# Small work of a graph kernel's last attention batch placed in pieces, its closing stage scaled two batches ahead, and the last batch normalised by halves

## The chip, the cores and the metric

The kernel runs on one core of a Trainium2 chip. The core has five engines that run side by side, each with its own instruction stream: TensorE (PE, matrix products; its weight loads are listed as PEld), VectorE (DVE), ScalarE (ACT), GpSimd (POOL) and SyncE (SP), which here only issues transfers. Sixteen DMA engines move data between HBM and the on-chip memory (SBUF); products of PE land in PSUM, a small second memory whose banks have to be freed before PE can write them again. Engines wait for one another through semaphores.

The metric is the device time of one execution in microseconds (us). Where several runs are given, it is their median.

## The reference

There are B = 16 batches of N = 1024 nodes with C = 256 features, all in fp32, and one dense adjacency matrix of 1024 x 1024. The computation has two layers, each with a residual and a layer normalisation over the features. Cut to what matters:

```python
# layer 0: graph-weighted queries, four heads of attention
g    = relu(einsum('bcn,bnm->bcm', fea, adj * A_s) * para)   # queries
k, v = split(x @ kv_w)
attn = softmax(q @ k.T * scale)                              # per head, 1024 x 1024
x    = layernorm(x + attn @ v)

# layer 1: graph convolution, two linear maps with batch norm
A_hat = normalise(adj + I)                                   # by degrees
agg   = einsum('nm,bmd->bnd', A_hat, x)
h     = relu(batchnorm(agg @ W1.T + b1))                     # statistics over all batches
out   = batchnorm(h @ W2.T + b2)                             # statistics over all batches
x     = layernorm(x + out)
```

The second batch norm needs its statistics over all sixteen batches before any batch can be finished. So the closing stage, which scales, adds the residual, normalises and stores, begins only when the last batch's second linear map is done.

## The kernel before

**How it is tiled.** A batch's features are a tile of 128 partitions x 8 node blocks x 256 features. Attention scores are made transposed, for two heads at a time, as tiles `ps` of 128 keys x 1024 (two heads x 512 queries). ACT makes `p` of them with an exponential, DVE adds up `acc` (the softmax's denominator), and PE multiplies `p` with `v` into `po`.

**What sets the order.** On PE, ACT and DVE the order of instructions is that of the program text (`manual_schedule`). On POOL and SP a scheduler orders what the text issues. In the attention, work is cut into *bursts* of two score tiles: in burst u of batch b (16 bursts in a batch) PE makes the scores of burst u, then `back(j - 1)` makes the products `po` of the burst before, with the DVE sums of `acc`. What follows in the burst is other work, in three kinds of lists:

- `sums`, the denominators of two heads (`normalise`): PE product `den`, ACT copy, two small transfers out to HBM and back as columns `dcol`.
- `full`, the residual of half the queries of two heads (`residual`): DVE reciprocal, PE transposes `poT`, DVE product `o`, POOL addition into `x`.
- `late`, the layer norm of a finished batch: `statistics_x1` (8 pairs of `bn_stats` and `bn_aggr` on DVE, then four POOL steps that give `rs_l` and `nm_l`) and `finish_x1` (8 ACT operations, line 622, then POOL issues the store to `x1_d`).

In the last batch, b = 15, there is no following batch whose queries could be prepared. Its bursts hold what the next layer needs (table `last`): transposes of the adjacency (`pah`, copied by ACT to `ahT`), loads and transposes of the weights (`pw1`, `pw2`, copied by DVE to `w12T`), node degrees (`dg`), whose inverse root makes a round trip through HBM to become `dinv_row`, and DVE's scaling of the adjacency rows with it (line 1107). The text also loads there the first batches of layer 0's result, `x1l_0` and `x1l_1`. Those take slots of the three-slot pool `xp`, and `x1l_1` gets the slot of batch 14's `x`. After the last burst PE goes over to the first aggregation, `pagg` (line 1134).

The transposes `pw`, `pah`, `poT` and `den` take turns in two PSUM banks (`tile_t`); `po` takes turns in two others, which are free when ACT's copy and DVE's addition into `oT` (lines 962, 963) are done.

**The closing stage.** `o2T[b]` holds batch b's output of the second linear map, with channels on partitions, in two blocks c. `batchnorm` gives the closure `coefficients` that makes scale `sg` and shift `sh` of one block: one DVE step and five POOL steps. Then, for each batch:

- `scale_shift(b)`: ACT scales and shifts `o2T[b]`, in place (line 1594).
- `residual2(b)`: PE transposes it back. Node blocks 0 to 3 go to PSUM tiles `pf` and DVE adds the residual; for blocks 4 to 7, PE itself adds the residual, in PSUM tiles `held`, of which there are three. DVE takes statistics of all eight blocks, and ten small operations on POOL (on DVE for the last batch) make `rstd` and `nmr` in a tile `w_l`.
- `finish(b)`: DVE normalises blocks 0 and 1, ACT blocks 4 to 7, 2 and 3; SP issues the store, and then loads the residual of a later batch into the freed place.

The loop runs `residual2(b)`, `scale_shift(b + 1)`, `finish(b - 1)`.

Of the kernel before, what the change touches and what calls it, by code (L numbers as in the profile page):

```python
# [18 lines left out]
P = 128  # L19
# [496 lines left out]
def fast_path(  # L516
# [87 lines left out]
    def layernorm_steps(t, name):  # L604


        st = small.tile([P, NCH, 6], F32, tag="ln_st", name=f"st_{name}")
        mv = small.tile([P, NCH, 2], F32, tag="ln_mv", name=f"mv_{name}")
        rstd = small.tile([P, NCH], F32, tag="ln_rs", name=f"rs_{name}")
        nmr = small.tile([P, NCH], F32, tag="ccol", name=f"nm_{name}")  # L610

        def statistics():
            for n in range(NCH):
                nc.vector.bn_stats(st[:, n, :], t[:, n, :])
                nc.vector.bn_aggr(mv[:, n, :], st[:, n, :])
            rsqrt(rstd, mv[:, :, 1], EPS)
            nc.gpsimd.tensor_tensor(nmr, mv[:, :, 0], rstd, ALU.mult)
            nc.gpsimd.tensor_scalar(nmr, nmr, -1.0, None, ALU.mult)  # L618

        def apply():  # L620
            for n in range(NCH):
                nc.scalar.activation(  # L622
                    t[:, n, :], t[:, n, :], AF.Identity,
                    bias=nmr[:, n : n + 1], scale=rstd[:, n : n + 1],
                )

        return statistics, apply
# [97 lines left out]
    with (  # L725
# [286 lines left out]

        def statistics_x1(b):
            statistics, st[b]["ln"] = layernorm_steps(st[b]["x"], f"l0_{b}")
            statistics()

        def finish_x1(b):
            s = st.pop(b)
            s["ln"]()
            nc.gpsimd.dma_start(x1_d[b], s["x"])  # L1020

# [20 lines left out]

        def transpose_weights():
            t = pap.tile([P, CC, N], F32, tag="pa", name="w12T")
            wl["w1T"] = t[:, 0, :].rearrange("p (c f) -> p c f", f=FH)
            wl["w2T"] = t[:, 1, :].rearrange("p (k c) -> p k c", c=C)
            for c in range(CC):
                pt = tile_t(f"pw1_{c}")
                for r in range(HC):
                    nc.tensor.transpose(  # L1050
                        pt[:, r * P : (r + 1) * P], wl["w1"][:, r, c * P : (c + 1) * P], ident
                    )
                nc.vector.tensor_copy(wl["w1T"][:, c, :], pt)
            for pair in range(HC // 2):
# [98 lines left out]
        with tc.manual_schedule(engines={mybir.EngineType.PE, mybir.EngineType.Activation, mybir.EngineType.DVE}):  # L1153
# [35 lines left out]
            for u, todo in (  # L1189
                (1, (load_weights,)), (6, (load_x1l, 0)), (9, (degrees,)), (10, (transpose_weights,)),  # L1190
                (12, (add_identity,)), (13, (load_x1l, 1)), (14, (scale_adjacency, 0)),
                (14, (scale_adjacency, 1)),
            ):
                last.setdefault(u, []).append((todo[0], todo[1:]))
            before_last = {
                8: [(adjacency_rows, (n,)) for n in (0, 1, 2, 3)],
# [6 lines left out]
            for j in range(len(bursts)):  # L1203
# [11 lines left out]
                if b == B - 1:  # L1215
                    if u == 0:
                        run(sums, 1)
                    elif u in (2, 9, 13):
                        run(full, 2)
                    elif u == 8:  # L1220
                        run(sums, 1)
                    elif u == 11:
                        run(late, 1)
                    elif u == 12:
                        run(late, 1)
                elif u == 0:
# [58 lines left out]

    def batchnorm(stats, gamma, beta, k, name):

# [5 lines left out]
        def coefficients(j):  # L1293
            g, s = sg[:, j : j + 1], sh[:, j : j + 1]
            nc.vector.bn_aggr(mv[:, j, :], stats[:, j].rearrange("p a s -> p (a s)"))
            rsqrt(g, mv[:, j, 1:2], EPS)
            nc.gpsimd.tensor_tensor(g, g, gamma[:, j : j + 1], ALU.mult)
            nc.gpsimd.tensor_tensor(s, mv[:, j, 0:1], g, ALU.mult)
            nc.gpsimd.tensor_tensor(s, beta[:, j : j + 1], s, ALU.subtract)

# [199 lines left out]
    with tc.tile_pool(name="hl", bufs=2) as hl, tc.tile_pool(name="o2p", bufs=1) as o2p:  # L1500
# [9 lines left out]

        coefficients2, sg2, sh2 = batchnorm(bn2_st, cols["g2"], cols["be2"], CC, "bn2")
        hs_of = {0: h0}
# [61 lines left out]
        with (  # L1574
# [14 lines left out]

            def scale_shift(b):  # L1590
                for hs in (H0, H1) if b == 0 else (slice(0, N),):
                    for c in range(CC):
                        o = o2T[b][:, c, hs]
# [14 lines left out]

            def residual2(b, between):
                xt = xf[b]  # L1610
                st = small.tile([P, NCH, 6], F32, tag="ln_st", name=f"st_l1_{b}")
                for pair in range(2):
# [10 lines left out]
                    for n in (2 * pair, 2 * pair + 1):  # L1623
                        nc.vector.bn_stats(st[:, n, :], xt[:, n, :])
                for pair in range(2, 4):
                    if b:
# [10 lines left out]
                for n in range(4, NCH):  # L1637
                    nc.vector.bn_stats(st[:, n, :], held[b][:, (n - 4) * C : (n - 3) * C])
                if b == B - 1:
                    between()  # L1640

                me, qe, mo, qo = (st[:, :, k] for k in (1, 2, 4, 5))
                w = small.tile([P, 4, NCH], F32, tag="ln_w", name=f"w_l1_{b}")
                rstd, nmr, dif, var = (w[:, k, :] for k in range(4))
                pool = nc.vector if b == B - 1 else nc.gpsimd
                pool.tensor_tensor(nmr, me, mo, ALU.add)
# [5 lines left out]
                pool.tensor_tensor(var, var, dif, ALU.add)  # L1652
                nc.gpsimd.tensor_tensor(rstd, var, mhalf, ALU.pow)
                pool.tensor_tensor(nmr, nmr, rstd, ALU.mult)
                pool.tensor_scalar(nmr, nmr, -0.5, None, ALU.mult)
                return rstd, nmr

            def finish(b, rstd, nmr):
                xt, hx = xf.pop(b), held.pop(b)
                y = o2T[b].rearrange("p c n -> p (c n)").rearrange("p (n c) -> p n c", c=C)  # L1660
                last = b == B - 1
                for n in (0, 1, 2, 3) if last else (0, 1):
                    nc.vector.tensor_scalar(
                        y[:, n, :], xt[:, n, :], rstd[:, n : n + 1], nmr[:, n : n + 1],
                        ALU.mult, ALU.add,
                    )
                for n in (4, 5, 6, 7) if last else (4, 5, 6, 7, 2, 3):
                    nc.scalar.activation(  # L1668
# [15 lines left out]
            add_x1(0, 3)  # L1684
            scale_shift(0)
            coeffs = {}
            for b in range(B):
                def before(b=b):
                    if b:
                        finish(b - 1, *coeffs.pop(b - 1))  # L1690

                coeffs[b] = residual2(b, before)
                if b + 1 < B:
                    scale_shift(b + 1)
                    before()
            finish(B - 1, *coeffs.pop(B - 1))
# [43 lines left out]
```

## Time and profile before

| | us |
|---|---|
| median of 3 runs | 2622.54 |
| their lowest and highest | 2620.62, 2622.65 |
| the profiled execution | 2621.04 |
| its span, first to last instruction | 2619.1 |

| engine | busy us | share of the span |
|---|---|---|
| PE | 2563.1 | 98% |
| DVE | 1516.7 | 58% |
| ACT | 1201.4 | 46% |
| POOL | 358.5 | 14% |

The granted clock of PE was 0.997 of full speed over the span. The stages lie in order of time: layer 0 up to about 1705 us, the aggregation and first linear map up to about 2297, the second linear map up to 2517, the closing stage to the end.

A line of a timeline reads: start in us, duration in us, engine, line of the kernel, operation, output <- input, shape, count; in brackets the time the engine was idle before it and what ended that wait. Neighbouring instructions of a kind are merged. In a table of waits the three numbers are the total in us, how often, and the longest.

### The profile page before, as it was taken

The numbers are of one execution on the slowest core, as the hardware profiler recorded it, in microseconds if no ns is written. First come the engines' busy times: TensorE is split into PE (matmuls) and PEld (weight loads), VectorE is DVE, ScalarE is ACT, GpSimd is POOL, SyncE is SP. The second block draws the span as 40 slices with busy tenths as digits, with TensorE's granted clock in tenths as the row PEclk, the third lists the DMA queues.
The fourth block names the chain that finished last, engine by engine and source line by source line (L and its number), as shares of the span: only waits on it lengthen the run. The fifth ranks groups of instructions, "written<-read, shape, count | busy, mean of one in ns | idle before, by whom it ended". The sixth has DMA issues, their size and how long they took to land. (4 is left out here: it accounts for less than half of the span.)

```text
span 2619.1 us, 32333 instructions
## 1 busy us (share of the span) xinstructions
PE 2563.1 (98%) x13158; PEld 1128.8 (43%) x13158; DVE 1516.7 (58%) x1952; ACT 1201.4 (46%) x1479; POOL 358.5 (14%) x430
## 2 busy tenths in 40 slices
PE   9999999999999999999999999899999999999987
PEld 5443443444434434444344444344444444444455
DVE  5375665655756646556566466676565565533367
ACT  6365564664665646646656564511100111133358
POOL 0010110101101101011011010232221122000035
PEclk9999999999999999999999999999999999999999
DMA  4001101011011011010110110112212222344458
GB/s 145 1 10 41 33 10 41 23 20 40 2 41 33 9 41 33 10 41 2 41 33 10 41 48 3 41 64 81 96 72 89 81 96 96 116 192 146 157 188 312
DMA packets 134574, 168.97 MB, mean 65 GB/s; under 512 B 86800, under 2 KB 120080, under 8 KB 124048
## 3 DMA queue, kind: packets, MB, share of 16 engines
q1 hardware_dynamic: 129056, 115.95, 14.2%
q0 software_dynamic: 4832, 50.34, 4.6%
q8 instruction: 105, 1.72, 0.3%
q10 hardware_dynamic: 528, 0.52, 0.1%
q14 instruction: 53, 0.43, 0.1%
HBM read 99.36 MB, written 67.44 MB: 64 GB/s over the span
## 5 line engine op out<-in xcount | busy, mean ns | idle before, releaser
L929 ACT ACTIVATE p<-ps 128x1024 f32<-128x1024 f32 x512 | 496.7, 1023 | 189.0 <-PE ps L924 159.3
L955 DVE TENSOR_TENSOR acc<-acc,p 128x1024 f32<-128x1024 f32 x384 | 484.9, 1263 | 126.8 <-ACT p L929 98.3
L924 PE MATMUL ps<-qT,kT 64*64 64x512 f32 x4096 | 491.8, 593 | 4.2 <-ACT p L929 3.8
L945 PE MATMUL po<-p,v 64*64 64x512 f32 x4096 | 489.8, 590 | 1.0 <-DVE oT L963 1.0
L827 PE MATMUL pg<-wg,x 128*128 128x512 f32 x960 | 420.9, 594 | 0.0
L945 PEld LDWEIGHTS po<-p,v 64*64 64x64 f32 x4096 | 160.4, 133 | 283.2 <-issue 272.7
L1011 POOL TENSOR_TENSOR x<-x,o 128x512 f32<-128x512 f32 x64 | 121.2, 1894 | 1157.3 <-DVE o L1006 1156.4
L924 PEld LDWEIGHTS ps<-qT,kT 64*64 64x64 f32 x4096 | 152.2, 133 | 285.2 <-issue 249.4
L827 PEld LDWEIGHTS pg<-wg,x 128*128 128x128 f32 x960 | 178.9, 190 | 221.5 <-issue 208.5
L1530 PE MATMUL po<-hl,w12T 128*128 128x512 f32 x512 | 220.0, 592 | 0.8 <-ACT hw L1482 0.8
L836 DVE SCALAR_TENSOR_TENSOR qT<-pg,para_s 128x1024 f32<-128x1024 f32 (+1 forms) x34 | 39.2, 1161 | 236.7 <-PE pg L827 235.0
L817 DVE SCALAR_TENSOR_TENSOR wg<-wg,adj_s 128x1024 f32<-128x1024 f32 x128 | 162.1, 1278 | 21.2 <-ACT wg L813 21.2
L808 ACT ACTIVATE wg<-crow,ccol 128x1024 f32<-128x1024 f32 x128 | 147.1, 1150 | 7.4 <-DMA crow<-c 7.4
L1530 PEld LDWEIGHTS po<-hl,w12T 128*128 128x128 f32 x512 | 97.2, 190 | 123.6 <-issue 119.8
L813 ACT ACTIVATE wg<-wg 128x1024 f32<-128x1024 f32 x128 | 136.2, 1065 | 1.7
L1467 ACT ACTIVATE hl<-hl,bn_sh,bn_sg 128x1024 f32<-128x1024 f32 x64 | 74.1, 1229 | 132.9 <-DMA hl<-h 131.5
L877 PE MATMUL pv<-kvw_s,xT 128*128 128x256 f32 x512 | 126.8, 390 | 6.7 <-ACT kT L868 6.7
L963 DVE TENSOR_TENSOR oT<-po,oT 128x512 f32<-128x512 f32 x64 | 44.2, 691 | 146.0 <-ACT oT L962 146.0
L864 PE MATMUL pk<-xT,kvw_s 128*128 128x512 f32 x256 | 121.9, 598 | 3.3 <-ACT v L882 3.3
L1558 DVE TENSOR_SCALAR o<-po,col_b 128x1024 f32<-128x1024 f32 x31 | 39.8, 1284 | 133.3 <-PE po L1530 133.3
L622 ACT ACTIVATE x<-x,nm_l,rs_l 128x256 f32<-128x256 f32 x128 | 64.6, 587 | 113.8 <-POOL nm_l L618 113.8
L839 ACT ACTIVATE qT<-qT 128x1024 f32<-128x1024 f32 (+1 forms) x34 | 34.1, 1007 | 175.2 <-DVE qT L836 175.2
(176 smaller groups left out, 2751.2 us busy)
## 6 DMA issues: line engine op xcount, KB each, us to landing
h<-hw POOLq DMA_DIRECT2D x16, 2048.0 KB, 6.7
hl<-h SPq DMA_DIRECT2D x15, 2048.0 KB
x<-x POOLq DMA_DIRECT2D x16, 1024.0 KB, 4.2
x1l<-x SPq DMA_DIRECT2D x16, 1024.0 KB
xf<-x SPq DMA_DIRECT2D x16, 1024.0 KB
x<-in_x_dram SPq DMA_DIRECT2D x15, 1024.0 KB
out_dram<-o SPq DMA_DIRECT2D x15, 1024.0 KB
crow<-c SPq DMA_DIRECT2D x15, 512.0 KB
```

Source lines behind the costliest of these rows:

```text
L808: nc.scalar.activation(w, s["crow"], AF.Abs, bias=s["ccol"][:, n : n + 1])
L813: nc.scalar.activation(w, w, AF.Tanh, scale=0.5)
L817: nc.vector.scalar_tensor_tensor(w, w, 1.0, adj_s[:, n, :], op0=ALU.subtract, op1=ALU.mult)
L827: nc.tensor.matmul(s["pg"][:, hs], xt[:, n, c * P : (c + 1) * P], s["wg", n][:, hs], start=(n == 0), stop=(n == NCH - 1),)
L864: nc.tensor.matmul(ps, kvw_s[:, c, kc * P : (kc + 1) * P], s["xT"][:, c, hs], start=(c == 0), stop=(c == CC - 1),)
L877: nc.tensor.matmul(pt[:, j * C : (j + 1) * C], s["xT"][:, c, n * P : (n + 1) * P], kvw_s[:, c, C : 2 * C], start=(c == 0), stop=(c == CC - 1),
L924: nc.tensor.matmul(ps[kh * D : (kh + 1) * D, hd * HALF : (hd + 1) * HALF], kT[r, pr, ks], qT[r, pr, qh * HALF : (qh + 1) * HALF], start=Tr ...
L929: nc.scalar.activation(p, ps, AF.Exp)
L945: nc.tensor.matmul(g["po"][kh][hd * D : (hd + 1) * D, :], s["v"][r, m, h * D : (h + 1) * D], p[r, hd * HALF : (hd + 1) * HALF], start=(m = ...
L955: nc.vector.tensor_add(g["acc"], g["acc"], p)
L1011: nc.gpsimd.tensor_tensor(xs, xs, o.rearrange("p n h d -> p n (h d)"), ALU.add)
L1530: nc.tensor.matmul(pss[c][:, hs], w2T[:, k, c * P : (c + 1) * P], h[k][:, hs], start=(k == 0), stop=(k == HC - 1),)
```

## The change

In the last batch's bursts:

- `statistics_x1` and `finish_x1` take a range of node blocks. Batch 14's statistics run two blocks at a time in bursts 6 to 9 (before: all in burst 11); its normalising runs in pieces of 2, 3 and 3 blocks in bursts 13, 14 and 15 (before: all in burst 12). POOL's steps follow the last piece of the statistics, the store the last piece of the normalising.
- The residual of batch 14's second pair of heads moves from burst 9 to burst 5.
- `transpose_weights` is cut in two: `pw1` stays in burst 10, `pw2` goes to burst 11.
- `load_x1l(1)` moves from burst 13 to the end of burst 15.

In the closing stage:

- For the second batch norm, four of the five POOL steps of `coefficients` run on DVE; the power stays on POOL. For the first one they stay on POOL.
- Batches 0 and 1 are scaled at the start, block c = 0 of both before block c = 1 of both. In the loop `scale_shift(b + 2)` takes the place of `scale_shift(b + 1)`.
- The ten small operations become a function `coefficients(b, st, ns, pool)`. For the last batch it is called twice, for node blocks 0 to 3 ahead of the statistics of blocks 4 to 7, and for blocks 4 to 7 after them; the last two steps run on POOL there too. Both calls stand ahead of `finish(14)`.
- In the last batch DVE normalises block 7 too, and ACT blocks 4 to 6.

The core of the diff:

```diff
-        def statistics():
-            for n in range(NCH):
+        def statistics(ns=range(NCH)):
+            for n in ns:
                 nc.vector.bn_stats(st[:, n, :], t[:, n, :])
                 nc.vector.bn_aggr(mv[:, n, :], st[:, n, :])
+            if NCH - 1 not in ns:
+                return
             rsqrt(rstd, mv[:, :, 1], EPS)
...
-                (1, (load_weights,)), (6, (load_x1l, 0)), (9, (degrees,)), (10, (transpose_weights,)),
-                (12, (add_identity,)), (13, (load_x1l, 1)), (14, (scale_adjacency, 0)),
+                (1, (load_weights,)), (6, (load_x1l, 0)), (9, (degrees,)),
+                (10, (transpose_weights, 0)), (11, (transpose_weights, 1)),
+                (12, (add_identity,)), (14, (scale_adjacency, 0)),
                 (14, (scale_adjacency, 1)),
             ):
                 last.setdefault(u, []).append((todo[0], todo[1:]))
+            for i in range(4):
+                ns = range(2 * i, 2 * i + 2)
+                last.setdefault(6 + i, []).append((statistics_x1, (B - 2, ns)))
+            for u, ns in ((13, range(2)), (14, range(2, 5)), (15, range(5, NCH))):
+                last.setdefault(u, []).append((finish_x1, (B - 2, ns)))
+            last[15].append((load_x1l, (1,)))
...
-                    elif u in (2, 9, 13):
+                    elif u in (2, 5, 13):
                         run(full, 2)
                     elif u == 8:
                         run(sums, 1)
-                    elif u == 11:
-                        run(late, 1)
-                    elif u == 12:
-                        run(late, 1)
+                    elif u == 3:
+                        late.clear()
...
             nc.vector.bn_aggr(mv[:, j, :], stats[:, j].rearrange("p a s -> p (a s)"))
-            rsqrt(g, mv[:, j, 1:2], EPS)
-            nc.gpsimd.tensor_tensor(g, g, gamma[:, j : j + 1], ALU.mult)
-            nc.gpsimd.tensor_tensor(s, mv[:, j, 0:1], g, ALU.mult)
-            nc.gpsimd.tensor_tensor(s, beta[:, j : j + 1], s, ALU.subtract)
+            eng.tensor_scalar(g, mv[:, j, 1:2], EPS, None, ALU.add)
+            rsqrt(g, g, 0.0)
+            eng.tensor_tensor(g, g, gamma[:, j : j + 1], ALU.mult)
+            eng.tensor_tensor(s, mv[:, j, 0:1], g, ALU.mult)
+            eng.tensor_tensor(s, beta[:, j : j + 1], s, ALU.subtract)
...
+                if last:
+                    first = coefficients(b, st, M0, nc.vector)
                 for pair in range(2, 4):
...
-                if b == B - 1:
-                    between()
...
+                if last:
+                    return first, coefficients(b, st, M1, nc.vector)
+                return (coefficients(b, st, slice(0, NCH), nc.gpsimd),) * 2
...
-                nc.gpsimd.tensor_tensor(rstd, var, mhalf, ALU.pow)
-                pool.tensor_tensor(nmr, nmr, rstd, ALU.mult)
-                pool.tensor_scalar(nmr, nmr, -0.5, None, ALU.mult)
-                return rstd, nmr
+                rsqrt(rstd, var, 0.0)
+                nc.gpsimd.tensor_tensor(nmr, nmr, rstd, ALU.mult)
+                nc.gpsimd.tensor_scalar(nmr, nmr, -0.5, None, ALU.mult)
+                return w[:, 0], w[:, 1]
...
-            scale_shift(0)
+            for c in range(CC):
+                scale_shift(0, (c,))
+                scale_shift(1, (c,))
             coeffs = {}
             for b in range(B):
-                def before(b=b):
-                    if b:
-                        finish(b - 1, *coeffs.pop(b - 1))
-
-                coeffs[b] = residual2(b, before)
-                if b + 1 < B:
-                    scale_shift(b + 1)
-                    before()
+                coeffs[b] = residual2(b)
+                if b + 2 < B:
+                    scale_shift(b + 2)
+                if b:
+                    finish(b - 1, *coeffs.pop(b - 1))
             finish(B - 1, *coeffs.pop(B - 1))
```

## The prediction

> **What bounds the kernel now.** I began with the page's busy line, where TensorE (PE) is busy for 98% of the span, so a saving must be a place where PE waits or the stretch in which it does not bind. The table of waits, for PE alone, says how little PE waits, and for what (us in total, times, longest):
>
> ```profile
> PE pf L1617 <- ACT o L1594: 10.6, 15, 2.3
> ...
> PE ps L924 <- ACT p L929: 3.8, 2, 3.6
> ...
> PE pw L1059 <- DVE w12T L1053: 2.7, 1, 2.7
> ...
> PE po L945 <- DVE oT L963: 1.0, 1, 1.0
> ```
>
> The last three fall within 22 us, in the last bursts of the attention. PE's timeline there (start, us):
>
> ```profile
> 1672.11 1.09 PE L1050 MATMUL pw<-ident,wl 128*128 128x128 f32 x8
> 1675.90 1.25 PE L1059 MATMUL pw<-ident,wl 128*128 128x128 f32 x8 [2.70 <-DVE w12T L1053]
> ...
> 1689.56 1.09 PE L1002 MATMUL poT<-ident,oT 128*128 128x128 f32 x8
> 1694.21 2.94 PE L924 MATMUL ps<-qT,kT 64*64 64x512 f32 x16 [3.56 <-ACT p L929]
> 1696.91 2.66 PE L945 MATMUL po<-p,v 64*64 64x512 f32 x16
> ...
> 1704.66 7.13 PE L1134 MATMUL pagg<-ahT,x1l 128*128 128x512 f32 x16
> ```
>
> The wait of 3.56 has its cause on ACT, in the same stretch: eight normalisings stand before the exponentials and themselves wait for GpSimd's (POOL's) coefficients.
>
> ```profile
> 1689.22 4.04 ACT L622 ACTIVATE x<-x,nm_l,rs_l 128x256 f32<-128x256 f32 x8 [4.30 <-POOL nm_l L618]
> ```
>
> The first line of the table belongs to the end, after 2517 us. Windows by stretch (PE, PEld, DVE, ACT, POOL busy, PE clock, DMA share, GB/s) show that there ACT binds, with the DMA engines as full:
>
> ```profile
> 2550.00:2560.00 10.00, 8.78 (x56) 6.58 (x55) 9.11 (x24) 10.00 (x17) 7.07 (x20) 1.00 0.99 356
> ...
> 2600.00:2604.00 4.00, 3.50 (x20) 2.55 (x21) 3.93 (x11) 3.25 (x7) 2.64 (x9) 1.00 0.56 190
> ```
>
> ACT's timeline of the end shows its only long gaps, one ahead and two behind:
>
> ```profile
> 2522.31 6.75 ACT L1594 ACTIVATE o<-o,bn_sh,bn_sg 128x512 f32<-128x512 f32 x7 [2.90 <-POOL bn_sh L1299]
> 2533.48 1.93 ACT L1668 ACTIVATE o<-held,w_l 128x256 f32<-128x256 f32 x4 [4.42 <-POOL w_l L1655]
> ...
> 2605.40 1.93 ACT L1668 ACTIVATE o<-held,w_l 128x256 f32<-128x256 f32 x4 [2.15 <-POOL w_l L1655]
> 2607.21 1.09 ACT L1668 ACTIVATE o<-xf,w_l 128x256 f32<-128x256 f32 x2
> 2610.33 1.93 ACT L1668 ACTIVATE o<-held,w_l 128x256 f32<-128x256 f32 x4 [2.03 <-DVE w_l L1655]
> 2612.29 0.43 ACTq L1675 DMA_DIRECT2D out_dram<-o  x1
> ```
>
> **Part one, the last batch's bursts.** A burst (16 `ps` and 16 `po` matmuls) starts every 3.43 us (1680.57 to 1684.00). From 1672.11 to the first `pagg` at 1704.66 are 32.55 us; the work in it is five bursts, a last `po` group of 1.72 and three groups of eight transposes at 1.02: 17.15 + 1.72 + 3.06 = 21.93. So 10.6 us can go: the waits of 2.70, 0.95 and 3.56, and 3.4 of slow matmuls around them (the burst from 1694.21 took 5.19).
>
> What the change does to each. The second half of `pw` goes one burst later, when DVE has copied the first: 2.70 goes. The 16 statistics operations (4.25 us on DVE in one block from 1680.26) become four groups of 1.06 in bursts 6 to 9, where DVE has 1.5 us or more free beside its 1.2 us `acc` additions: the wait of `po` for `oT` goes. The eight normalisings go as 2, 3, 3 to bursts 13 to 15. Their coefficients are ready near 1675 (POOL took 4.5 us after the statistics), ten us before. A piece of three is 3 x 0.505 = 1.5; ACT is idle for 1.48 in each burst, and its exponentials end 1.2 us before PE needs their banks (1565.6 against 1566.88), so 3.56 goes and nothing takes its place.
>
> What it costs. The residual moved from burst 9 to 5 now stands before adjacency transposes, as its twin in burst 2 does: there PE waits 0.35 and 0.78 for the same PSUM tiles, so +1.1. In burst 14 DVE has two `acc` and two row scalings (2.5 + 2.5 against 3.43), and PE no longer waits for it: I follow DVE to the `oT` addition at about 1698, where `pagg` wants its bank at 1696.7. Nothing before shows this wait; bounds are 0 and 2.5, I take 1.4. The load of `x1l_1` goes from burst 13 to 15, behind the same store (store issued at 1693.55 before, load at 1698.39; now about 1694 and 1699), and is wanted by PE near 1726: hidden, with 20 us to spare. POOL's x1S sums wait for it, and end near 1713, again before 1726. On SP one denominator load now stands behind the `dinv` store, which waits for POOL until 1670; it is wanted near 1684. `dinv_row` (13 us from POOL's power to landing before) lands near 1683; DVE wants it at 1691. Sum: 10.6 - 1.1 - 1.4 = **8.1 us**.
>
> Here a rule speaks against the move to burst 5. The row first: in burst 2, eight `poT` and eight `pah` transposes with 1.13 of waiting are followed by 16 `ps` matmuls in the usual 1.95, at clock 1.00. The Trainium skill (TensorE: Matmul & The Clock Gate, Part 1 and Part 4) says that the clock halves after an idle window of about 3.4 us, and that transposes do not count as busy. By that, 2.2 of transposes and 1.1 of waiting are 3.3, at its edge, and a slow burst like that at 1694.21 (+1.8) could follow: the part would be 6.3. I take the row. The other half of the rule agrees with the removed stall (3.56 idle, then clock 0.66 in 1695 to 1700).
>
> **Part two, the start of the end.** For `bn2` four of five POOL steps per channel go to DVE. Before, the second channel's took 1.8 us (2520.51 to 2522.31); DVE's dependent small operations take 0.20, hand-overs 0.15, the power stays on POOL: about 1.7. DVE waits for work then. ACT's gap of 2.90 is filled by the first channel of batches 0 and 1 (2.4 us), so batch 0's second channel is done near 2523.4 rather than 2524.3, and its coefficients come near 2532.5 rather than 2533.44. In the gap of 4.42, ACT scales batch 3. It was ACT's next work after batch 0's normalising, so it is 2.3 off its later path: from there ACT is 3.2 ahead.
>
> **Part three, the run.** Per batch ACT needs 5.05 (six normalisings and two scalings), but batch 1 to 13 took 61.8/12 = 5.15, since PE waits for each scaling and every third coefficient is 0.17 late. Two ahead, both waits go: 12 x 0.10 = 1.2. DVE with 4.76 and POOL with 4.2 per batch stay below 5.05. By ACT's order, batch 12 is normalised at 2532.5 + 60.6 + 3.0 = 2596.1, 13 by 2599.1. Batch 14's coefficients: its PSUM tile is free at 2590.0 (batch 11), then PE 3.5, DVE 1.5, POOL 4.3: 2599.3; ACT ends it at 2602.5.
>
> **Part four, the last batch.** Its tile is free at 2595.0, PE is done at 2598.6, DVE adds seven small operations (1.0 us as at 2607.00) for the first half, which lie under POOL's work for 14; 1.35 of statistics, 1.0 again, to 2601.9; POOL's power over four columns is between 0.57 (one) and 1.65 (eight), I take 1.05, and with two POOL steps and hand-overs 2603.8. Three normalisings of 0.48 on ACT, the fourth on DVE: the last store is issued at 2605.3 instead of 2612.29: **7.0 us**.
>
> The transfers could forbid it. From 2535.5 on, nine loads and sixteen stores of 1.05 MB are 26.2 MB. The windows of 10 us from 2540 to 2590 give 349 to 404 GB/s (mean 373): 70.2 us, to 2605.7; the Trainium skill (DMA: Bandwidth & Descriptors, Specifications) puts a core's HBM limit at about 358: 73.2 us, to 2608.7. Before, data ended 3.75 after the last issue (2616.05), so ACT's schedule wants 2609.05. The trace went above the rule's figure; by both ACT ends last, by the rule just so.
>
> **Sum.** 8.1 + 7.0 = 15.1 from this execution's 2621.04: 2605.9. The median shown is 1.5 higher, so I say **2607**.
>
> **Rivals.** *Only the end pays* (13%): DVE becomes the bound in bursts 12 to 15, what PE gains it waits for at `pagg` and `b_agg`; DVE's lag there speaks for it, its idle 14 us between 1660 and 1696 against: 2622.5 - 7.0 - 1 = 2614.5. *Transfers bind the end* (16%): at the 346 GB/s of stores alone (2610 to 2612), 26.2 MB take 75.8 us, data end near 2612, the end gives 4: 2610.5. *Both small* (6%): each gap moves on, within 0.2% (5.2 us), about the smallest difference that can be told from none here. *Slower* (5%): `x1l_1`, now loaded after the last normalising, comes late and stalls PE at its first product; it decides from 1726, and is slower than before from 1741, 37 us behind the store where now it takes 10: say 2630. That the moves don't take place is out: the order on PE, ACT and DVE is written by hand. The forecast has 60%.
>
> The first three cases lie in 2601 to 2615, with a low end where the two guessed waits do not come and the power is shorter. Faster: 0.60 + 0.13 + 0.16 = 0.89; same 0.06; slower 0.05.
>
> **What would show it.** Right: first `pagg` near 1696; no PE wait above 1.5 between 1665 and 1700 and a clock of 1.00 there; new waits of `pah` in burst 5; ACT without gaps from 2532 to 2599; the last ACT store about 83 us after the first scaling of the second channel (90 before). Wrong: a PE wait for DVE at `pagg` above 3, exponentials late in bursts 14 and 15, a DMA share of 1 up to the end, `pf` still waiting for ACT.

## The result, and the profile after

| | before | after |
|---|---|---|
| median of 6 runs each, us | 2622.41 | 2612.05 |
| lowest and highest | 2620.62, 2622.65 | 2610.89, 2612.64 |
| the profiled execution | 2621.04 | 2612.64 |
| its span | 2619.1 | 2610.6 |

The changed kernel takes 0.9962 of the time before (95% interval 0.9949 to 0.9974): 10.4 us less, where 15.1 were forecast. Of the kernel after, the slowest of its six runs was profiled; of the kernel before, one of the faster. So the two traces are only 8.4 apart, and sums on traces go by that.

The table of waits of the kernel after, PE alone (total us, times, longest). Two of the four lines shown of before are gone (`ps` for `p`, apart from a usual 0.3, and `pw` for `w12T`), `pf` for ACT went from 10.6 to 1.9, and `po` for `oT` has changed its name: it is `pagg` now that wants the bank.

```profile
PE pagg L1139 <- DVE oT L965: 3.3, 1, 3.3
PE held L1614 <- ACT o L1686: 3.1, 8, 0.4
...
PE pf L1629 <- ACT o L1605: 1.9, 1, 1.9
```

PE's timeline of the kernel after (start, duration, ..., count, and in brackets the idle time before it), the bursts at 5 and the step to the aggregation:

```profile
1650.14 0.66 PE L1087 MATMUL pah<-ident,adj_s 128*128 128x128 f32 x4 [0.41 <-DVE o L1008]
...
1651.58 0.66 PE L1087 MATMUL pah<-ident,adj_s 128*128 128x128 f32 x4 [0.78 <-ACT ahT L1090]
1652.16 1.95 PE L926 MATMUL ps<-qT,kT 64*64 64x512 f32 x16
...
1695.45 2.84 PE L1139 MATMUL pagg<-ahT,x1l 128*128 128x512 f32 x6
1701.56 7.63 PE L1139 MATMUL pagg<-ahT,x1l 128*128 128x512 f32 x10 [3.27 <-DVE oT L965]
```

The first `pagg` comes 9.2 us sooner than before, as forecast (0.4 of that was there at the start of the last batch). But before, its sixteen matmuls ran in one piece of 7.13 us. Now they are cut after six, PE stands for 3.27, and the ten that follow take 7.63. In one piece sixteen cost 0.446 each, so ten ought to cost 4.5: 3.2 us more are lost to the clock. The windows of the kernel after show it (PE, PEld, DVE, ACT, POOL busy, granted clock of PE, DMA share, GB/s):

```profile
1702.00:1704.00 2.00, 2.00 (x3) 0.73 (x3) 2.00 (x3) 0.00 (x0) 0.00 (x0) 0.50 0.92 389
1704.00:1706.00 2.00, 2.00 (x4) 0.67 (x3) 2.00 (x2) 0.00 (x0) 1.05 (x1) 0.50 0.16 61
1706.00:1708.00 2.00, 2.00 (x4) 0.89 (x3) 2.00 (x2) 0.00 (x0) 2.00 (x2) 0.56 0.00 0
```

PE is listed as busy all through, at half the clock. What PE waited for is DVE, whose timeline of the kernel after shows it without a gap:

```profile
1692.42 2.47 DVE L1112 SCALAR_TENSOR_TENSOR ahT<-ahT,dg,dinv_row 128x1024 f32<-128x1024 f32 x2
1694.81 6.10 DVE L957 TENSOR_TENSOR acc<-acc,p 128x1024 f32<-128x1024 f32 x3
1700.83 0.68 DVE L965 TENSOR_TENSOR oT<-po,oT 128x512 f32<-128x512 f32 x1
```

Three additions into `acc` take 6.10 where two elsewhere take 2.54. The second of the three is the long one, and in just that time POOL makes the sums `wS` of the weights (DVE's timeline in that window, then POOL's):

```profile
1696.13 3.12 DVE L957 TENSOR_TENSOR acc<-acc,p 128x1024 f32<-128x1024 f32 x1
```

```profile
1696.06 0.74 POOL L686 TENSOR_TENSOR wS<-w12T 128x256 f32<-128x256 f32 x1
1696.75 0.73 POOL L688 TENSOR_TENSOR wS<-w12T 128x256 f32<-128x256 f32 x1
1697.43 0.72 POOL L687 TENSOR_TENSOR wS<-wS,w12T 128x256 f32<-128x256 f32 x1
1698.23 1.60 POOL L689 TENSOR_TENSOR wS<-w12T,wS 128x256 f32<-128x256 f32 x1
```

It is so in the whole trace: of the 384 additions `acc<-acc,p`, 362 have no addition of POOL (into `x`, or a sum `wS`) beside them, and none of these takes more than 1.23; of the 22 that have one, 19 take 1.56 to 3.12. The kernel before had sixteen of 2.10 to 2.11, one in each batch, beside POOL's additions into `x`; this one (DVE's timeline of before) lies in the last batch, beside one that runs from 1696.30 to 1698.48:

```profile
1697.46 2.10 DVE L955 TENSOR_TENSOR acc<-acc,p 128x1024 f32<-128x1024 f32 x1
```

The Trainium skill (SBUF — State Buffer, SBUF: two separate sides) has a rule that fits: a VectorE operation with two inputs in SBUF and a GpSimd operation that reads SBUF need the same pair of ports, and whichever starts first has it for its whole length while the other stands. If the addition that starts at 1696.13, 0.07 behind the first sum, stands for three sums, to 1698.15, and then needs its own 1.21, it ends at 1699.36 (an estimate from these lines). It ended at 1699.25. And POOL's fourth sum, from 1698.23, took 1.60 where the others took 0.73. Why the addition did not get its turn behind the first sum, no line shows.

At the end, ACT's timeline of the kernel after answers to the gaps of 2.90, 4.42 and 2.03 before:

```profile
2519.42 7.18 ACT L1605 ACTIVATE o<-o,bn_sh,bn_sg 128x512 f32<-128x512 f32 x7 [0.70 <-DVE bn_sh L1310]
2529.14 1.93 ACT L1686 ACTIVATE o<-held,w_l 128x256 f32<-128x256 f32 x4 [2.54 <-POOL w_l L1671]
...
2601.64 1.48 ACT L1686 ACTIVATE o<-held,w_l 128x256 f32<-128x256 f32 x3 [2.44 <-DVE o L1680]
2603.14 0.43 ACTq L1693 DMA_DIRECT2D out_dram<-o  x1
```

From the first scaling of the second channel to ACT's last store there are 83.72 us, 89.98 before. But the last gap, 2.44, is no shorter than the 2.03 before: ACT's coefficients are there at 2600.94, and it waits 0.7 more for DVE. (Of the ten small operations of the last batch, nine ran on DVE before; the power was on POOL then too.)

### The profile page after: what moved, and what is told of

Same layout as the page of the kernel before. It is cut to its first block, busy times and chain, and to the rows that moved or that the text cites. A ratio compares the mean times of both kernels' runs of the same rounds, so it can differ in the third digit from the quotient of the medians.

```text
span 2610.6 us, 32351 instructions
## 1 busy us (share of the span) xinstructions
PE 2561.6 (98%) x13158; PEld 1127.4 (43%) x13158; DVE 1518.4 (58%) x1966; ACT 1201.1 (46%) x1478; POOL 356.6 (14%) x427
## 4 chain that ended last, share of the span: by engine, by line
PE 86%; DVE 9%; ACT 3%; issue 1%; DMA 0%; POOL 0%; DVEq 0%; POOLq 0%; ACTq 0%
PE ps L926 16%; PE po L947 16%; PE pg L829 16%; PE po L1541 8%; PE pv L879 5%; PE b_agg L1371 4%; PE c_agg L1371 4%; PE pk L866 3%; PE a_agg L1371 2%; PE b_h L1403 2%; PE c_h L1403 2%; PE pxT L790 1%; PE den L977 1%; PE a_h L1403 1%; PE pagg L1139 1%; PE pg L851 1%
```

## The experiments

Two distances on each trace tell the parts of the program apart better than the medians do: from the start of the last batch (its first `den`) to the first `a_agg`, just behind `pagg`; and from there to ACT's last store. Seven profiles with `pagg`'s wait of 3.25 to 3.27 have its ten matmuls at 6.05 to 7.63, so medians of five runs cannot settle less than about 1 us. The bursts of before and of e2 are the same code, and their first distance differs by 0.7. And each set of runs had runs of before beside it, to which its ratios go, with medians of 2622.41 (e1 to e4), 2621.10 (e5 to e8) and 2621.32 (e9 to e12): between sets, medians may differ by some 1.3 for no reason in the kernel.

| kernel | median, us | ratio to before (95%) | `den` to `a_agg` | to last store |
|---|---|---|---|---|
| before | 2621.1 to 2622.4 | | 114.27 | 877.16 |
| after | 2612.05 | 0.9962 (0.9949 to 0.9974) | 112.07 | 870.61 |
| e1_bursts_only | 2617.06 | 0.9981 (0.9973 to 0.9989) | 110.69 | 875.66 |
| e2_end_only | 2615.30 | 0.9975 (0.9965 to 0.9985) | 115.01 | 870.51 |
| e3_ws_on_dve | 2609.65 | 0.9951 (0.9937 to 0.9965) | 107.62 | 870.50 |
| e4_scale_early | 2608.19 | 0.9946 (0.9932 to 0.9959) | 107.37 | 870.51 |
| e5_act_first | 2611.99 | 0.9965 (0.9951 to 0.9978) | 112.06 | 870.58 |
| e6_spread_act_first | 2606.99 | 0.9948 (0.9934 to 0.9962) | 106.09 | 870.91 |
| e7_one_piece | 2608.47 | 0.9952 (0.9938 to 0.9965) | 107.46 | 870.47 |
| e8_one_ahead | 2616.43 | 0.9982 (0.9975 to 0.9989) | 110.67 | 875.24 |
| e9_stats_one_block | 2611.57 | 0.9962 (0.9948 to 0.9975) | 110.64 | 870.52 |
| e10_bn2_on_pool | 2611.60 | 0.9962 (0.9948 to 0.9976) | 110.47 | 871.49 |
| e11_no_halves | 2611.99 | 0.9962 (0.9949 to 0.9976) | 110.53 | 869.94 |
| e12_spread_act_four | 2607.22 | 0.9944 (0.9931 to 0.9958) | 106.10 | 871.76 |

The theory at the start: DVE is late for `oT` because POOL's `wS` sums slow its addition, and the wait halves the clock behind it. Rivals: the store of batch 14, moving at some 400 GB/s then, slows DVE; DVE has too much to do there whatever POOL does; or the end is to blame for what is missing.

### The two halves alone: e1 and e2

e1 has the changed bursts and the closing stage of before, e2 the bursts of before and the changed closing stage.

> The changed bursts with the closing stage of before. Theory: the bursts reach the first aggregation product some 9 us sooner, but 6.5 of it is given back there (PE waits 3.3 for DVE's oT, then runs at half clock), so this kernel is 2 to 4 us faster than before: 2618.5 to 2620.5. Rival (the end brings nothing because the transfers bind it, all comes from the bursts): 10 us faster, 2612.

> The bursts of before with the changed closing stage. Theory: the end alone brings 6.5 to 7 us: 2615.5 to 2616. Rival (transfers bind the end): 0 to 2 us, 2620.5 to 2622.5. The two halves should add up to the 10.4 us of the whole change; if they do not, they act on one another.

e1 gained 5.4 by medians, e2 7.1. Their sum, 12.5, is 2.1 above what both bring together. In its trace e1's bursts gain 3.6 (114.27 to 110.69) and its closing stage, though unchanged, another 1.5: before's profile has the clock at 0.62 and 0.53 in 2524 to 2528, e1's at 1.00 throughout. And `pagg` stalls in e1 as in the kernel after, with a shorter bill:

```profile
1702.95 6.25 PE L1139 MATMUL pagg<-ahT,x1l 128*128 128x512 f32 x10 [3.25 <-DVE oT L965]
```

So the stall belongs to the bursts and the end delivers. What is missing from the sum is, by these traces, how long the clock stays low: the 1.5 of the end is counted in e1 and in e2, and `pagg` cost e1 1.4 less than the changed kernel. e1 came out 1.4 us faster than the theory's range for it, which left out that the clock of the end could recover; e2 came out 0.2 faster than its own.

### POOL's sums or the store: e3

```diff
         left_sums(
-            nc.gpsimd, [wS[:, i, :] for i in range(4)],
+            nc.vector, [wS[:, i, :] for i in range(4)],
```

> The changed kernel, but the four sums wS of the first linear map's weights, which POOL makes right after the last po product, are made by DVE where it waits for the aggregation's copies. Theory A (POOL's sums slow DVE's acc addition, which took 3.1 us instead of 1.2): the addition takes 1.2 to 1.4, oT is done near 1699, PE waits at most 1.5 at pagg and keeps its clock: 4 to 5 us faster than the changed kernel, 2607 to 2608. Theory B (the store of x_14, which runs at 426 GB/s in the same microseconds, slows DVE): the addition still takes about 3 us, wait and half clock stay: 2612.

DVE's and PE's timelines of e3:

```profile
1696.06 3.87 DVE L957 TENSOR_TENSOR acc<-acc,p 128x1024 f32<-128x1024 f32 x3
```

```profile
1701.46 4.53 PE L1139 MATMUL pagg<-ahT,x1l 128*128 128x512 f32 x10 [1.92 <-DVE oT L965]
```

With POOL silent, three additions take 3.87 instead of 6.10, though the store runs at 393 GB/s beside them (1698 to 1700). The store alone does not slow DVE; the sums on POOL do. Two of the sums landed ahead of `oT` on DVE (0.84 us), so 1.92 of the wait stay, but behind that wait the clock stayed at 1.00 and ten matmuls took 4.53. That is 4.5 us sooner at `a_agg`, of which 1.4 are wait and 3.1 clock. The median is only 2.4 lower than the changed kernel's, short of the 4 to 5 expected: the wait was 1.9 and not 1.5 at most, and the changed kernel's profile has the longest `pagg` of the seven; against the shortest, 6.05, the clock would give 1.5.

So the wait has two parts. Without the two sums on DVE, some 1.1 of e3's 1.92 would stay (an estimate: 1.92 - 0.84), and that is DVE's own lateness; the other 2.2 of the 3.27 are POOL's sums.

### DVE's work spread: e4, e6

e4 moves the degrees and the scalings out of DVE's way; e6 does so in a looser form and takes in e5's edit of the end.

```diff
-                (1, (load_weights,)), (6, (load_x1l, 0)), (9, (degrees,)),
+                (1, (load_weights,)), (6, (load_x1l, 0)), (7, (degrees,)),        # e4; e6: 8
...
-                (12, (add_identity,)), (14, (scale_adjacency, 0)),
-                (14, (scale_adjacency, 1)),
+                (10, (add_identity,)), (11, (scale_adjacency, 0)),                # e6: 10, 12
+                (12, (scale_adjacency, 1)),                                       # e6: 13
```

> The changed kernel, with degrees in burst 7 (from 9) and the two row scalings in bursts 11 and 12 (both from 14), so that DVE is not behind when the last po product ends. Theory (DVE's lateness, made by two scalings in burst 14, is what PE waits for; POOL's contention only lengthens it): oT is done before 1698, no wait at pagg above 0.5, clock 1.00 there: 6 us faster than the changed kernel, 2606. Rival 1 (the wait is set by contention alone, whatever DVE's order): 2611 to 2612. Rival 2 (dinv_row lands late and DVE stalls in burst 11 or 12, or the denominator columns come late behind it): 2612 or more, with a DVE wait for a DMA there.

> Degrees in burst 8, the identity in entry 10, the two row scalings one by one in bursts 12 and 13 (the changed kernel: 9, 12, both in 14), and ACT's blocks first as in e5. Theory: DVE has slack of 1 us and more in each of these bursts, so oT is on time at pagg (no wait, 16 pagg matmuls in 7.1 us, clock 1.00) without the waits of 1.9 us that the earlier form (degrees in 7, scalings in 11 and 12) had for den and acc; 6.5 us of the last burst come back, 0.6 at the end: 2605 (2604.3 to 2606.5). Rival: any place in these bursts costs PE its own wait, since DVE is late there by as much; then it stays where the earlier form was, 2608.

In e4 the sixteen `pagg` run in one piece of 7.13 again. But it gained 3.9, not 6: the degrees in burst 7 found their input not ready, and PE paid at `den` (76.89 from there to the first `pagg`, 74.99 in the changed kernel). DVE's and PE's timelines of e4:

```profile
1662.77 0.17 DVE L1097 TENSOR_TENSOR dg<-dg 128x8 f32<-128x8 f32 x1 [3.35 <-ACT ahT L1090]
```

```profile
1667.20 1.05 PE L977 MATMUL den<-acc,ones 128*32 128x512 f32 x4 [0.75 <-DVE acc L957]
```

One burst later these waits are gone. PE's timeline of e6, the only wait of the stretch and the step to the aggregation:

```profile
1695.25 1.09 PE L947 MATMUL po<-p,v 64*64 64x512 f32 x8 [0.24 <-ACT p L931]
1696.27 7.13 PE L1139 MATMUL pagg<-ahT,x1l 128*128 128x512 f32 x16
```

`a_agg` comes 6.0 us sooner than in the changed kernel, and the median is 5.1 lower (3.7 by the ratios to before), 14.1 us under before: with e12, which has the same bursts, the best version of the study. (The expectation's 2605 was 2 too low; its working counted 6.5 for the burst and 0.6 for e5's edit, which e5 shows to be worth nothing.) POOL's sums still run beside DVE here, from 1697.64, but DVE's last addition for `oT` had begun at 1696.84 and kept its 1.22. So the long wait needs both, a late DVE and the sums: with either taken away (e3, e4, e6) the clock held.

### One piece or three, one block or four: e7 and e9

e7 normalises batch 14 in one piece of eight in burst 13; e9 takes its statistics in one block in burst 8.

```diff
-            for u, ns in ((13, range(2)), (14, range(2, 5)), (15, range(5, NCH))):
+            for u, ns in ((13, range(NCH)),):                      # e7
...
-            for i in range(4):
-                ns = range(2 * i, 2 * i + 2)
-                last.setdefault(6 + i, []).append((statistics_x1, (B - 2, ns)))
+            last.setdefault(8, []).append((statistics_x1, (B - 2, range(NCH))))   # e9
```

> The normalising of batch 14 in one piece of eight in burst 13 (4.04 us on ACT) instead of 2, 3, 3 in bursts 13, 14, 15; all else as changed. If the pieces matter: ACT has 1.5 us of room in a burst and 1.2 of lead, so PE waits 1.3 us or more for the exponentials of burst 14, and what of it DVE uses to catch up comes off the 3.3 us wait at pagg: 2611 to 2613. If the clock goes with it (halved behind the wait), 2614 to 2616. Rival, that the statistics early were all that was needed and the pieces bring nothing: no PE wait for p above 0.5, 2612 with the same pagg wait of 3.3.

> Batch 14's sixteen statistics operations in one block of 4.25 us in burst 8, instead of 1.06 in each of bursts 6 to 9; all else as changed. If early is enough: DVE was idle 3.2 us ahead of the oT addition there and has slack in bursts 8 to 10, PE waits 0.5 us or less in them, and the time is that of the changed kernel, 2611.5 to 2612.8. Rival, that the cut is what pays: PE waits 2 to 3 us for an addition of DVE (po for oT, den for acc or ps for p) in bursts 8 to 10, as the 4.25 block did before the change: 2614 to 2615.

Both fell to the same side: cutting is not what pays. e9 is at the changed kernel's time, with no new wait of PE. e7 is 3.6 faster than the changed kernel, which no theory had. Its timeline of ACT, then of POOL, DVE and PE:

```profile
1685.78 4.03 ACT L624 ACTIVATE x<-x,nm_l,rs_l 128x256 f32<-128x256 f32 x8
1689.71 1.91 ACT L931 ACTIVATE p<-ps 128x1024 f32<-128x1024 f32 x2
```

```profile
1690.11 0.65 POOL L1023 DMA_DIRECT2D x<-x  x1 [0.97 <-ACT x L624]
...
1697.29 1.71 POOL L688 TENSOR_TENSOR wS<-w12T 128x256 f32<-128x256 f32 x1
```

```profile
1695.53 4.55 DVE L957 TENSOR_TENSOR acc<-acc,p 128x1024 f32<-128x1024 f32 x3
```

```profile
1700.73 4.56 PE L1139 MATMUL pagg<-ahT,x1l 128*128 128x512 f32 x10 [1.73 <-DVE oT L965]
```

The exponentials behind the piece of 4.03 are just in time: the first ended at 1690.72, and the next `ps` started at 1690.90 without a wait. My working gave ACT 1.5 us of room and 1.2 of lead; it left out that PE makes eight transposes in that burst (1.0 us), so ACT had about 3.7 for its 4.0. What stalled PE before was that the eight normalisings waited 4.30 for coefficients, not that they were eight. Counted from the first `den`, the store leaves six us sooner here. DVE's three additions take 4.55 beside the same sums, and now it is POOL that is slow: 1.71 for a sum that took 0.73. By the rule of the ports that is the same conflict with the turns dealt otherwise: here an addition was under way when POOL began at 1696.37, and from there the engines alternate. (An addition and a sum together took 1.66, less than 1.22 and 0.73 one behind the other, so not all of a listed length is time at the port.) Why three sums in a row went ahead of the addition in the changed kernel is open. DVE's addition into `oT`, which has one of its two inputs in PSUM, was not slowed by a sum beside it: it took its usual 0.68 (DVE's and POOL's timelines of e7).

```profile
1700.00 0.68 DVE L965 TENSOR_TENSOR oT<-po,oT 128x512 f32<-128x512 f32 x1
```

```profile
1698.95 1.71 POOL L687 TENSOR_TENSOR wS<-wS,w12T 128x256 f32<-128x256 f32 x1
```

That POOL's sums slow DVE is shown by e3; that the ports are the reason rests on these times, and no run changed the ports alone. PE's wait of 1.73 left the clock alone, as e3's 1.92 did.

### The end: e8, e10, e11, e5, e12

e8 scales one batch ahead in the loop; e10 puts the small steps of the second batch norm back on POOL; e11 normalises the last batch as one, ACT taking blocks 4 to 7; e5 puts ACT's blocks ahead of DVE's block 7; e12 is e6's bursts with the halves kept and ACT taking blocks 4 to 7.

```diff
-                if b + 2 < B:
-                    scale_shift(b + 2)
+                if 0 < b < B - 1:
+                    scale_shift(b + 1)                                     # e8
...
-        coefficients2, sg2, sh2 = batchnorm(bn2_st, cols["g2"], cols["be2"], CC, "bn2", nc.vector)
+        coefficients2, sg2, sh2 = batchnorm(bn2_st, cols["g2"], cols["be2"], CC, "bn2", nc.gpsimd)   # e10
...
-                if last:
-                    first = coefficients(b, st, M0, nc.vector)
...
-                if last:
-                    return first, coefficients(b, st, M1, nc.vector)
-                return (coefficients(b, st, slice(0, NCH), nc.gpsimd),) * 2
+                return (coefficients(b, st, slice(0, NCH), nc.vector if last else nc.gpsimd),) * 2   # e11
...
-                for n in (0, 1, 2, 3, 7) if last else (0, 1):
+                for n in (0, 1, 2, 3) if last else (0, 1):                 # e11, e12; e5: 7 after ACT's loop
-                for n in (4, 5, 6) if last else (4, 5, 6, 7, 2, 3):
+                for n in (4, 5, 6, 7) if last else (4, 5, 6, 7, 2, 3):     # e11, e12
```

> In the loop of the closing stage batch b + 1 is scaled instead of b + 2 (batch 1 at the start as changed); all else as changed. Theory (two ahead gives 1.2 us in the run and the 2.3 us filled gap at the start; the halves and bn2 the rest): 3.5 us slower than the changed kernel, 2615.6, and PE waits for o of scaling again, some 8 to 10 us in 13 or more. Rival: ACT's total work sets the end whatever the order: within 1 us of 2612, with the PE waits back but without effect.

> The second batch norm's small steps on POOL again as before the change; all else as changed. Theory: from DVE's bn_aggr to ACT's first scaling of the second channel 1.8 us instead of 1.43, and everything after it later by that: 0.4 us slower, 2612.4 (ratio 0.9965). Rival: ACT's first gap is filled by two batches' first channel anyway, no difference at all.

> The last batch is normalised as one: one set of coefficients for eight blocks, behind the statistics of all eight, steps on DVE and POOL as changed; DVE normalises blocks 0 to 3 and ACT 4 to 7. Worked out from the changed kernel's trace: statistics done 2597.9, seven DVE steps 1.0, POOL's power over eight columns 1.65 (four: 1.2), two steps 0.7, so coefficients near 2601.4 instead of 2600.9; ACT four blocks 1.93 at once, where it first waited 0.7 for DVE's block 7: the last store 0.3 us later (84.0 us after the first scaling of the second channel), 0.3 to 1 us slower with the first half's store: 2612.4 to 2613.0. Rival, that the halves are worth what the step says (the first half's work lies under other work): 1.5 us and more slower, 2613.5 to 2614.5.

> Only the order of the last normalising is changed: ACT's blocks 4 to 6 stand ahead of DVE's block 7 in the text. In the changed kernel ACT waited for DVE's block 7 (L1680, to 2601.64) after POOL's last coefficient (2600.94). Theory: the wait is for the text's order on the same coefficients and tile, so ACT now starts right behind POOL's step and the end is 0.6 us sooner: 2611.4 (ratio to the changed kernel 0.9998, inside the noise of the medians; it is read from the trace: ACT's last wait then names POOL, and from the first second-channel scaling to the last ACT store there are 83.1 us instead of 83.7). Rival: ACT was late through its own queue, and nothing moves: 83.7 us.

> The spread form (degrees in burst 8, scalings in 12 and 13) with ACT normalising all of blocks 4 to 7 of the last batch, DVE none of them; coefficients by halves as changed. In the changed kernel and with ACT first the two engines took turns on that PSUM tile (1.48 + 0.54 in a row), so the fourth block on DVE brought nothing; on ACT it is 0.45 more and no turn: the last store 0.2 us sooner, 83.5 us after the first scaling of the second channel, and 2606.8. Rival: ACT waits for something of DVE all the same, 83.9 and 2607.2.

**e8** is 4.4 us slower than the changed kernel. From the first scaling of the second channel to the last store it takes 88.45 us, as e1 did with the old end (88.50), against 83.7. PE's waits are back in the table of e8:

```profile
PE pf L1629 <- ACT o L1605: 10.8, 15, 2.0
```

So scaling two ahead carries the end's gain, 4.7 us, and the other edits of the end together add nothing to that distance when the loop scales one ahead (the second batch norm's steps lie ahead of it).

**e10** cannot be told from the changed kernel by its median. Its trace has the step as expected, 1.80 us from the last `bn_aggr` to ACT's scaling instead of 1.43; the clock also fell behind PE's wait (2.32 instead of 1.95), which made the distance 84.33.

**e11** was expected 0.3 us later at the last store and is 0.6 sooner, 83.11; the median shows no difference. DVE's timeline of the changed kernel and then of e11, the statistics of the last four blocks:

```profile
2596.33 0.16 DVE L1668 TENSOR_TENSOR w_l<-w_l 128x4 f32<-128x4 f32 x1
2596.41 1.42 DVE L1652 BATCH_NORM_STATS2 st_l<-held 128x6 f32<-128x256 f32 x4
```

```profile
2594.34 1.42 DVE L1650 BATCH_NORM_STATS2 st_l<-held 128x6 f32<-128x256 f32 x4 [0.22 <-PE held L1644]
...
2599.36 1.38 DVE L1676 TENSOR_SCALAR o<-xf,w_l 128x256 f32<-128x256 f32 x4 [1.83 <-POOL w_l L1667]
```

Counted from the first scaling of the second channel, the statistics start at 76.99 with halves and at 76.13 without: the first half's seven steps stand ahead of them on DVE, 0.86 us. The shorter power on POOL (1.19 instead of 1.69) gives 0.5 back, and the fourth block on DVE (ACT 1.48 instead of 1.93) another 0.45, but ACT waits 0.7 for that block. Together 0.6 lost. My working for e11 had taken the statistics' time from the changed kernel, with the first half's steps in it.

**e5** shows what that 0.7 is. ACT's and DVE's timelines of e5:

```profile
2600.80 1.48 ACT L1689 ACTIVATE o<-held,w_l 128x256 f32<-128x256 f32 x3 [1.78 <-POOL w_l L1671]
2602.96 0.42 ACTq L1698 DMA_DIRECT2D out_dram<-o  x1
```

```profile
2602.38 0.54 DVE L1681 TENSOR_SCALAR o<-held,w_l 128x256 f32<-128x256 f32 x1 [1.70 <-ACT o L1689]
```

ACT starts right behind POOL, as the theory had it, but now DVE waits for ACT, and the store waits for DVE: 83.71 us, unchanged. The two engines take turns, whichever is first in the text; they read one PSUM tile and write one output tile, and which of the two makes them wait was not tried. **e12** lets ACT do all four; its profile has 84.60, of which 1.09 is a clock of 0.59 and 0.55 at the start of the end (the gap ahead of batch 0's normalising is 3.63 there, 2.54 elsewhere). The 83.5 that are left agree with the expectation, but only after that subtraction; its median is the rival's number and does not tell it from e6. Normalising the last batch as one in e6's kernel, which e11 speaks for, was not tried.

## Why the prediction was right, and where it was too high

The time lies in the range, and both parts of the gain came by the ways forecast; but of 15.1 us only 10.4 came, since most of what the bursts freed was lost again at `pagg`. A wait there above 3 us for DVE was one of the prediction's own signs of being wrong, and it appeared. By number alone the result is nearer to the rival of the transfers (2610.5) than to 2607; the traces and the experiments decide between them. By the prediction's own steps, against the profiled executions:

| step | forecast | shown |
|---|---|---|
| stalls and slow matmuls up to the first `pagg`, less new waits of `pah` (10.6 - 1.1) | 9.5 | 8.8 (`den` to first `pagg`: 83.80 before, 74.99 after) |
| `pagg` waits for `oT` | -1.4 (0 to -2.5) | -6.6 (first `pagg` to `a_agg`: 30.47 before, 37.08 after) |
| the end, to the last store | 7.0 | 6.3 (89.98 to 83.72) |

- **The failed step is the wait of `pagg`.** I followed DVE to the `oT` addition "at about 1698", with additions of 1.2 us each. It came at 1700.83, because POOL's `wS` sums ran beside DVE and one addition took 3.1. DVE's own lateness, about 1.1 by the estimate at e3, was priced well with 1.4; the 2.2 of the sums and the clock behind the wait (1.6 to 3.2 in the seven profiles) were put at nothing. The profile of before had the warning sixteen times: an addition of 2.1 beside POOL's addition into `x`, one of them shown above. I counted the instructions that the change brings next to `pagg` on DVE, and not those of POOL beside them; the rule of the shared ports, quoted above, would have said to. The bound of 2.5 was too tight by 0.8, and no price was put on the clock behind such a wait, though the removed stall of 3.56 had shown one (the burst behind it took 1.8 us longer). In this profile and e5's the clock cost as much as the wait, in the five others half of it.
- **The clock rule.** At burst 5 I took the trace's row against the rule of the Trainium skill (TensorE: Matmul & The Clock Gate, Part 1 and Part 4), and the row held: waits of 0.41 and 0.78 among the transposes, then sixteen `ps` in 1.95. Where the rule would have been of use is the `pagg` wait: 3.25 to 3.27 halved the clock in all seven profiles that have it, 1.73 and 1.92 in neither. The page puts the idle window at about 3.4; by these numbers less is enough, 3.25 every time here, and at the start of the closing stage once 1.95 (e12), with a wait of 1.36 some 2 us ahead of it.
- **The moves of part one.** The stalls of PE went, but those of 0.95 and 3.56 not by the cuts: with the statistics in one block (e9) or the normalising in one piece (e7) they are gone too. That both run early is enough. Taking out both cuts at once was not tried, nor the split of `transpose_weights` (the stall of 2.70) or the residual's move alone. And the 3.4 us of slow matmuls that the sum counted were not all the clock's: in the windows of before it stands at 1.00 from 1684 to 1694, so only the 1.8 behind the last stall are.
- **Hidden as forecast:** the load of `x1l_1`, issued at 1700.19, holds up POOL for 5.1 us and PE never. The rival that it comes late is out.
- **The end.** The lead of two batches in the loop was worked out as 2.3 and 1.2, and is worth 4.7. The second batch norm's steps gave 0.37 where 0.1 was taken. The halves of the last batch, on which part four leaned, cost 0.6 together with its fourth block on DVE. Yet the sum came close, and that is in part luck: 1.5 of the 6.3 is the clock that before's profile lost at 2524 to 2528 and e1's, with the same code, did not, so the forecast counted as a gain what may or may not occur in an execution. (The clock fell behind PE's wait of 2.32 in two profiles of three, and behind the changed kernel's 1.95 in one of eleven, so the shorter wait may have earned a part of the 1.5; three profiles don't show it.) From the last store to the end of the execution it took 9.5 us, 8.75 before, which takes 0.75 back; what takes it was not tried.
- **Transfers binding the end** is out as the main limit: ACT's order sets the last store, no wait of PE, DVE or ACT after 2519 names a DMA in the kernel after, and the order of scaling alone moved the last store by 4.7 (e8). But it was close: the DMA engines' share was 1.03 and 1.04 from 2602 to 2606, at 338 and 342 GB/s.
- **That only the end pays** would have needed the bursts to give nothing; they gave 3.6 in e1's trace, and 8.2 once DVE's work was spread (e6, 114.27 to 106.09).

## What to carry to other kernels

When work is moved beside other work, look at what the *other* engines run in that time as well: an addition on DVE of 1.2 us took 3.1 beside POOL's sums, and no count of DVE's own instructions shows it. A wait of PE of 3.3 us cost one and a half times to twice its length here, because matmuls behind it ran at half the clock, while waits of 1.7 and 1.9 at the same place cost only themselves; a forecast that allows a long wait has to price both. And take the stretch of before's profile that a gain is worked out from and ask whether it is the program's or that execution's: a clock loss of 1.5 us stood in this one, and a second profile of the same code was without it.

## What was unexpected of the hardware

- The turns of DVE and POOL at their shared ports may fall either way for one and the same work: three of DVE's additions took 6.10 beside sums of 0.73 (after), or 4.55 beside sums of 1.71 (e7).
- At the start of the closing stage the clock fell or not in runs with the same wait: after PE's 2.32 in before and e10 but not in e1, after 1.95 in e12 but in none of the ten other profiles that have it. Behind the same wait of 3.25 to 3.27 ten matmuls took from 6.05 to 7.63. No run here tells what decides it.
